# Another slot list for the first pair of a mixture-of-experts layer, with GpSimd's weight combinations moved

## The chip, the cores and the metric

The kernel runs on one core of a Trainium2 chip. A core has a matrix engine (TensorE, PE in the profile; its weight loads are PEld), a vector engine (VectorE, DVE), a scalar engine (ScalarE, ACT), GpSimd (POOL) and a sync engine (SP) that here only issues DMAs. Each engine works through its own queue in order; semaphores make one wait for another. The metric is the device time of one execution in microseconds (us), the median of several.

## The reference

All in float32. B = 8 samples, T = 512 tokens, H = 256; 64 context rows a sample; E = 3 experts with hidden width 512.

```python
nx = layer_norm(x, ln_gamma, ln_beta)
q, k, v = nx @ Wq, context @ Wk, context @ Wv
weights = softmax(q @ k.T * H ** -0.5)
evidence = weights @ v
combined = concatenate([nx, evidence, broadcast(cond)], axis=-1)
router_probs = softmax(combined @ router_W + router_b)
h = silu(einsum('btc,ecr->bter', combined, e_w1) + e_b1)
expert_out = einsum('bter,erh->bteh', h, e_w2) + e_b2
routed = sum(expert_out * router_probs[..., None], axis=-2)
g = sigmoid(silu(combined @ gate_w1 + gate_b1) @ gate_w2 + gate_b2)
return x + g * (routed @ out_w + out_b)
```

## The kernel before

The eight samples go in four pairs. For a pair, a layer's two samples and two halves of the features form a 2 by 2 block product, which is done with seven products in place of eight (Strassen's scheme with Winograd's sums). The operands of the seven are sums of activations (tile `T`) and sums of weights (`ws`, `gw2s`, `w2s`). The sums of weights are made on GpSimd by `combine` (lines 250 to 253, four operations each): `combine_weights(g)` for the first layers, `combine_gate` for the gate's second layer, `combine_second` for the experts' second layer. That second layer is multiplied beforehand by `out_w` into `w2o`: this is done once, in the first pair, by `transpose_second` (VectorE) and `second_layer` (TensorE, ScalarE), six units.

`gate_layer(j)` makes the gate's first layer of pair j up to the sums of x. Then `half_layers(j)` makes the experts' first layers (groups n = 1 to 6) and finishes the gate (n = 0). Its products are cut in two halves of 64 rows of the matrix engine, which run side by side on its upper and lower half. The order is written out by hand: a list of 57 slots, each with one product for each half, and behind the bar the steps that other engines are given at that point. The first pair has a list of its own, `SLOTS_0`, because it also holds set-up work; then `UNITS_0`, steps around the six units; then `LATE_0`, three groups of steps run in `outputs`. `HOME_0` names the bank of PSUM of each sum (eight banks). A sum that takes over a bank must wait until the earlier one has been read.

The tokens: `P1.3` is product 1 of group 3, `U`, `V`, `Y`, `Z`, `W` the parts from the evidence. `k` copies a sum (ScalarE, line 886), `a` adds one to h (VectorE, line 883), `s` is the silu (ScalarE, line 877), `w` weighs h with the router's probabilities `pb` (VectorE, line 920), `df` subtracts one weighed block from another (line 917). `lp` and `lg` are the x part of the router's logits of this pair and of the next (line 638), `rl` their evidence part (lines 751, 754), `rs` and `rx` add them up and take exponents, and `r` makes the probabilities and sends them out: `spread_probabilities` writes them to DRAM with four DMAs (`pd`, line 796) and reads them back spread over all partitions with one (`pb`, line 800), all from GpSimd's queue. `g0` to `g3` are sums for the gate's second layer (line 1229), `b2` prepares a bias (lines 564 to 569), `lx` loads the next pair's x, `st`, `dev`, `nm` are its statistics, deviation and normalization (lines 581, 585, 595), `xd` and `xg` store and reload it, `l1` and `l2` load the second weights of experts 1 and 2, `t0` to `t5` transpose them, `xb` loads x for the output. `c2` and `cg` are `combine_weights(2)` and `combine_gate`.

Each of these calls only appends instructions to its engine's queue. A GpSimd step, say, runs as soon as GpSimd's queue reaches it and its operands are there, whatever slot it is written in; the place in the list sets the order within each queue. In the setup, `end_softmax` gives GpSimd a copy of one column of the softmax's result (`wake_t`) ahead of its next work, so that this work starts after the softmax.

Of the kernel before, what the change touches and what calls it, by code (L numbers as in the profile page):

```python
# [8 lines left out]
F32 = mybir.dt.float32  # L9
# [7 lines left out]
def kernel(  # L17
# [51 lines left out]
    nc = tc.nc  # L69
    P = 128  # L70
    B, T, H = x.shape
    CT = context.shape[1]
    E, C3, RH = e_w1.shape
    KH = H // P
# [25 lines left out]
    def bank(i, name):  # L100
        ps = psum.tile([P, 512], F32, tag=f"b{i}", name=name)
        bank_of[ps.name] = i
        return ps

    def spares(*banks):
        spare[:] = banks
# [11 lines left out]
    eps_t = const.tile([P, 1], F32, tag="eps_t", name="eps_t")  # L118
    warm_t = const.tile([P, 1], F32, tag="warm_t", name="warm_t")

    wake_t = const.tile([P, 1], F32, tag="wake_t", name="wake_t")

    def load_table(func):
        nc.scalar.activation(warm_t, warm_t, func)
# [73 lines left out]
    r = 0  # L198
# [263 lines left out]

    def late_anchors():

        ps = bank(1, "ps_ar")
        for g in range(E):
            turned(ps, condT, wa[g], g * P)
        turned(ps, b2T, ow_sb, E * P)
        blocks = work.tile([P, T], F32, tag="yb", name="ar_blocks")
        n = E * P + KH * QB  # L470
        nc.vector.transpose(blocks[:, :n], ps[:, :n])
        for g in range(E):
            ar[g] = blocks[:, g * P : (g + 1) * P]
        ar["b2"] = blocks[:, E * P : n]
# [61 lines left out]

    def second_layer(u):
        e, i = u // 2, 2 * (u % 2)
        ps = bank((4, 7, 6, 5)[u % 4], f"ps_w2o_{u}")
        for d in range(2):  # L540
            for k in range(KH):
                c = k * H + d * P
                nc.tensor.matmul(  # L543
                    ps[:, d * H : (d + 1) * H], w2["T"][u % 2][:, c : c + P], ow_sb[:, k, :],
                    start=(k == 0), stop=(k == KH - 1),
                )
        c = e * RC + i
        nc.scalar.copy(w2o[:, c : c + 2, :].rearrange("p c n -> p (c n)"), ps)
        if i:
            combine_second(e)  # L550
# [371 lines left out]
    def gate_layer(j, steps):  # L922
# [96 lines left out]
    }  # L1019

    SLOTS_0 = (
        "P1.1 Z.1 |",
        "Y.1 Z.0 |",
        "P1.3 P1.1 | lp0.0 a10.0",
        "Y.0 W.0 | k00.1 lp0.1 s10.0 lp0.2",
        "P2.1 P1.3 | w11.0",
        "P4.0 P5.1 | a00.0 k00.3 s11.0 lp0.3",
        "P6.1 P2.1 | lp1.0 s00.0 lp1.1",
        "P5.1 Z.2 | a00.1",
        "U.0 P6.1 | lp1.2 k11.1 lp1.3 lx l1 l2 c2 cg s00.1",  # L1030
        "P1.2 P5.2 | rl k10.1",
        "Y.2 P4.0 | b2",
        "P5.2 P1.2 | s01.0",
        "P2.3 P3.1 | k00.2 k11.2 rs",
        "P7.1 V.1 | g0 rx",
        "P2.2 Z.3 | st0.0 st0.1",
        "P6.2 P7.1 | st0.2 st0.3",
        "Y.3 P5.3 | a11.1",
        "P3.1 P6.2 | r s11.1",
        "P6.3 V.2 | st1.0 k10.2 a10.1",  # L1040
        "P5.3 P3.2 | st1.1 s10.1",
        "U.1 P2.2 | st1.2 k11.3 st1.3",
        "P3.2 P2.3 | a00.2 dev",
        "P1.6 P6.3 | g1 a00.3",
        "P7.2 P3.3 | a10.2",
        "P4.1 P1.6 | g2",
        "P2.4 P7.2 | g3 k10.3 nm0.0 k00.6",
        "P1.5 P4.1 | nm0.1 a11.2 s00.2",
        "P1.4 V.3 | nm0.2 s01.1 nm0.3 xd0",
        "P7.3 P1.5 | nm1.0 s00.3 nm1.1 nm1.2 s10.2",  # L1050
        "P3.3 P1.4 | nm1.3 xd1 xg w00.1 k00.5",
        "P6.6 Z.6 | a10.3 k00.4",
        "P4.2 P7.3 | s11.2 w10.1 w11.1 s10.3",
        "U.2 P6.6 | a11.3",
        "P6.5 Z.4 | k10.6 w00.2 s11.3 w01.1",
        "P6.4 P4.2 | w00.3",
        "Y.4 P6.5 | s01.2 w10.2",
        "U.3 P6.4 | w11.2 k10.5 w10.3",
        "P4.3 P2.4 | k10.4 w11.3",
        "Y.6 P5.4 | a00.4 w01.2",  # L1060
        "P7.5 P4.3 | s00.4 lg0.0",
        "P5.4 P5.6 | w00.4 s01.3 lg0.1",
        "P7.4 Z.5 | k11.4 w01.3",
        "P5.6 P5.5 | lg0.2 lg0.3",
        "Y.5 P7.4 | lg1.0 k11.6 lg1.1",
        "P5.5 P7.5 | lg1.2 a11.4",
        "P2.5 P3.4 | k11.5 lg1.3 s11.4 df.1",
        "P7.6 V.6 | a11.5 t0",
        "P2.6 P3.6 | w11.4 s11.5",
        "U.4 V.5 | df.2 w11.5",  # L1070
        "P3.6 P7.6 | df.3",
        "U.5 P3.5 | a11.6 a10.6 t1",
        "P4.5 V.4 | s11.6 s10.6 w11.6",
        "P4.4 P2.5 | w10.6",
        "U.6 P4.5 | a00.5",
        "P4.6 P4.4 | s00.5 s01.5",
        "P3.4 P2.6 | w00.5 s01.4 w01.5",
        "P3.5 P4.6 | a00.6",
    )
    UNITS_0 = (  # L1080
        "a10.4 s01.6 s10.4",
        "t2 a10.5 s00.6",
        "w01.4 t3 s10.5 xb0 xb1",
        "w01.6 w00.6 t4",
        "w10.4 t5",
        "w10.5",
    )
    LATE_0 = ("", "", "df.6 df.4 df.5")
    HOME_0 = {
        "U.0": 0, "Z.0": 2, "Y.0": 3, "W.0": 1, "U.1": 4, "Z.1": 5, "Y.1": 6, "U.3": 7, "Z.2": 2,  # L1090
        "U.2": 1, "Y.2": 3, "Y.3": 6, "Z.3": 0, "U.6": 5, "Y.4": 3, "U.5": 6, "U.4": 2, "Z.6": 4,
        "Z.4": 0, "Y.6": 1, "Z.5": 3, "Y.5": 7,
    }

    def half_layers(j):
# [23 lines left out]
        def half(token, k):  # L1119
# [21 lines left out]
            "rs": lambda: router_logits(j),  # L1141
            "rx": lambda: router_exp(j),
            "b2": lambda: second_bias(),
            "c2": lambda: combine_weights(2),
            "cg": lambda: combine_gate(),
            "lx": lambda: [load_x(b) for b in (2, 3)],
            **{f"l{e}": lambda e=e: load_second(e) for e in range(1, E)},
# [60 lines left out]
                step(token)  # L1208
        if not j:
            for u, tokens in enumerate(UNITS_0):  # L1210
                second_layer(u)
                for token in tokens.split():
                    step(token)
        S["late", j] = [lambda t=tokens: [step(x) for x in t.split()] for tokens in late]

    gate_sums = {}
# [207 lines left out]
    with tc.manual_schedule(engines=None):  # L1424
# [63 lines left out]
        def end_softmax():  # L1488
            sum_weights(0)
            softmax(0)  # L1490
            nc.gpsimd.tensor_copy(wake_t, S["w", 0][:, 0, 0, 0:1])
            value_differences(0, 0)
            turn_weights(0)
            anchor_columns(E)
            combine_x(0, nc.vector, (3,))
            combine_weights(0)
            router_column()
            spread_router_bias()
            spread_router_rows(0)
            combine_weights(1)  # L1500

        def end_setup():
            value_differences(0, 1)
# [5 lines left out]
        for j in range(NP):  # L1509


            within, between = {}, {}

            def put(where, n, step, *args):
                where.setdefault(n, []).append(lambda: step(*args))

            spares(7, 5)
            if j == 0:
                spares(4, 5, 7)
                copies = []  # L1520

                def value_product(g):
                    value_weights(0, g, lambda *args: copies.append(args), False)

                def copy_values():
                    nc.scalar.copy(*copies.pop(0))

                put(within, 1, value_product, 0)
                put(within, 1, begin_softmax)
                put(within, 5, copy_values)  # L1530
                put(within, 6, load_table, AF.Silu)
                put(within, 3, value_product, 1)
                put(within, 3, copy_values)
                put(within, "sums", end_softmax)
                put(within, 7, value_product, 2)
                put(within, 7, copy_values)
                put(within, 7, end_setup)
            else:
                put(within, 3, value_weights, j, 1, nc.scalar.copy, False)
            if j + 1 < NP:  # L1540
                b0, b1 = 2 * j + 2, 2 * j + 3
                if j + 2 < NP:
                    put(between, "begin", load_x, b0 + 2)
                    put(between, "begin", load_x, b1 + 2)
                put(between, "begin", transpose_blocks, b0)
                put(between, "gate", regroup_x, b1)
                put(between, "begin", value_weights, j + 1, E)
                put(between, "begin", store_router_rows, j + 1)
                put(between, "begin", spread_router_rows, j + 1)
                put(between, "P5", transpose_blocks, b1)  # L1550
                put(between, "P6", value_weights, j + 1, 2)
                put(between, "P2", scores, j + 1)
                put(between, "P2", exponents, j + 1)
                put(between, "P2", combine_x, j + 1, nc.gpsimd)
                put(between, "P7", softmax, j + 1)
                put(between, "P7", value_weights, j + 1, 0)
                put(between, "P7", evidence_logits, j + 1)
                put(between, "P7", router_logits, j + 1)
                put(between, "P3", turn_weights, j + 1)
                put(between, "P3", router_exp, j + 1)  # L1560
            gate_layer(j, within)
            half_layers(j)
            outputs(j, between)

# [33 lines left out]
```

## Time and profile before

| what | us |
|---|---|
| median of 3 runs | 461.6 (460.97 to 461.93) |
| the profiled execution, own time | 461.67 |
| its span, first to last instruction | 459.3 |
| TensorE busy in the span | 451.5 |
| VectorE busy | 364.0 |
| ScalarE busy | 214.1 |
| GpSimd busy | 100.7 |
| first pair: first slot of its list starts | 33.99 |
| first pair: second weights' units start | 87.20 |
| first pair: the gate's second layer starts | 98.16 |

The span is what the profiler's instruction records cover; the execution's own time has in addition what lies before and after. Times in a profile row are the start from the beginning of the span and the duration. In brackets stands the idle time of the engine before the row and what ended it: `[1.05 <-DVE h L883]` is 1.05 us of idle ended by VectorE's operation of line 883 that wrote h. A row with x8 merges eight like instructions. The records of matmuls overlap by their pipeline, so a matmul of 0.59 us is followed by the next after 0.43.

### The profile page before, as it was taken

How to read it: one execution, taken by the hardware profiler on the slowest of the kernel's cores; microseconds unless marked ns; L12 is line 12 of the kernel's file. 1: busy time of each engine (PE TensorE's matmuls, PEld its weight loads, DVE VectorE, ACT ScalarE, POOL GpSimd, SP SyncE). 2: the span in 40 equal slices, each digit the busy share in tenths (PEclk: the TensorE clock that was granted, in tenths of full speed). 3: DMA queues.
4: the chain of work that ended last, by engine and by line, in shares of the span. 5: the costliest groups of instructions: out<-in, count | busy, mean ns of one | idle time of the engine just before them, and what ended most of it. 6: DMA issues, size and time to landing. Idle time of an engine off the chain costs nothing.

```text
span 459.3 us, 5502 instructions
## 1 busy us (share of the span) xinstructions
PE 451.5 (98%) x1797; PEld 216.6 (47%) x1797; DVE 364.0 (79%) x683; ACT 214.1 (47%) x373; POOL 100.7 (22%) x148
## 2 busy tenths in 40 slices
PE   8999989999999999999999999999999999999996
PEld 7544346664444444444444444444444444444445
DVE  2879989958689999479779999678869837677983
ACT  2545675556221576468220476568130456558000
POOL 5458500081062400001053300001044300000010
PEclk9999999999999999999999999999999999999999
DMA  8975572262011377403011368102011381000014
GB/s 261 385 158 125 91 230 47 47 137 46 7 23 23 48 233 124 103 0 47 7 23 23 48 204 138 28 0 46 7 23 23 48 213 17 1 0 0 1 16 76
DMA packets 119379, 35.31 MB, mean 77 GB/s; under 512 B 106012, under 2 KB 116312, under 8 KB 118840
## 3 DMA queue, kind: packets, MB, share of 16 engines
q1 hardware_dynamic: 115344, 27.02, 29.0%
q0 software_dynamic: 2080, 7.16, 4.7%
q10 hardware_dynamic: 1928, 0.80, 0.6%
q8 instruction: 14, 0.23, 0.2%
q14 instruction: 13, 0.11, 0.1%
HBM read 27.56 MB, written 7.39 MB: 76 GB/s over the span
## 4 chain that ended last, share of the span: by engine, by line
PE 90%; DMA 4%; DVE 3%; SPq 1%; issue 1%; POOL 0%; DVEq 0%; POOLq 0%
PE ps_u L841 40%; PE ps_z L841 19%; PE ps_y L841 12%; PE ps_vw L816 5%; PE ps_gu L841 3%; PE ps_w2o L543 2%; DMA pb<-pd 2%; PE ps_s L687 2%; PE ps_gz L841 1%; DMA scr_w<-in_L_xcond_Wv_dram 1%; PE ps_tokens L841 1%; PE ps_v L352 1%; PE ps_m L352 1%; PE ps_gy L841 1%; DVE junk L638 1%
## 5 line engine op out<-in xcount | busy, mean ns | idle before, releaser
L841 PE MATMUL ps_u<-nxT,w 64*128 64x512 f32 (+1 forms) x208 | 96.7, 591 | 0.0
L920 DVE TENSOR_TENSOR h<-h,pb 128x512 f32<-128x512 f32 x96 | 63.8, 696 | 18.0 <-ACT h L877 12.1
L877 ACT ACTIVATE h<-h,abias 128x512 f32<-128x512 f32 x72 | 49.5, 717 | 34.5 <-DVE h L883 34.5
L841 PE MATMUL ps_u<-h,w2o 128*128 128x512 f32 x144 | 64.2, 595 | 0.0
L841 PE MATMUL ps_z<-wT,vw 64*128 64x512 f32 x104 | 52.4, 591 | 1.3 <-DVE h L883 1.3
L841 PE MATMUL ps_z<-nxT,ws 64*128 64x512 f32 (+1 forms) x104 | 52.4, 590 | 0.0
L841 PE MATMUL ps_z<-T,ws 64*128 64x512 f32 (+1 forms) x104 | 51.6, 591 | 0.0
L841 PE MATMUL ps_y<-nxT,w 64*128 64x512 f32 (+1 forms) x104 | 51.5, 590 | 0.0
L1329 POOL TENSOR_TENSOR yb<-yb,xb 128x512 f32<-128x512 f32 x14 | 17.7, 1266 | 148.7 <-DVE yb L1328 131.6
L841 PEld LDWEIGHTS ps_u<-nxT,w 64*128 64x128 f32 (+1 forms) x208 | 37.0, 187 | 25.7 <-issue 22.6
L841 PE MATMUL ps_u<-T,ws 64*128 64x512 f32 (+1 forms) x104 | 48.7, 591 | 0.0
L841 PE MATMUL ps_u<-T,w 64*128 64x512 f32 x112 | 48.7, 589 | 0.0
L841 PE MATMUL ps_z<-h,w2s 128*128 128x512 f32 x96 | 42.5, 592 | 0.0
L841 PEld LDWEIGHTS ps_u<-h,w2o 128*128 128x128 f32 x144 | 27.0, 190 | 32.7 <-issue 30.9
L886 ACT COPY h<-ps_u 128x512 f32<-128x512 f32 x48 | 27.6, 579 | 22.6 <-PE ps_u L841 22.6
L1296 DVE TENSOR_TENSOR h<-h,h 128x1024 f32<-128x1024 f32 x24 | 34.3, 1485 | 0.0
L429 POOL DMA_DIRECT2D vrd<-vw x8 | 5.0, 627 | 114.2 <-ACT vw L823 111.6
L841 PE MATMUL ps_u<-wT,vw 64*128 64x512 f32 x56 | 28.3, 594 | 1.1 <-DVE h L883 1.1
L841 PEld LDWEIGHTS ps_z<-h,w2s 128*128 128x128 f32 x96 | 18.2, 190 | 23.0 <-issue 22.3
L841 PE MATMUL ps_y<-wT,vw 64*128 64x512 f32 x56 | 28.3, 595 | 0.0
L816 PE MATMUL ps_vw<-w,vT 128*128 128x512 f32 (+1 forms) x64 | 26.7, 539 | 0.0
L841 PEld LDWEIGHTS ps_y<-nxT,w 64*128 64x128 f32 (+1 forms) x104 | 19.4, 187 | 13.6 <-issue 13.4
(230 smaller groups left out, 822.6 us busy)
## 6 DMA issues: line engine op xcount, KB each, us to landing
pb<-pd POOLq DMA_DIRECT2D x4, 1536.0 KB, 7.4
xb<-in_x_dram SPq DMA_DIRECT2D x64, 64.0 KB, 2.4
out_dram<-yb SPq DMA_DIRECT2D x56, 64.0 KB, 1.9
x<-in_x_dram SPq DMA_DIRECT2D x24, 128.0 KB, 2.9
xd<-x SPq DMA_DIRECT2D x24, 128.0 KB, 2.2
xg<-xd SPq DMA_DIRECT2D x48, 64.0 KB, 2.3
w<-in_L_xcond_e_w_dram SPq DMA_DIRECT2D x4, 512.0 KB, 6.8
scr_wa<-in_L_xcond_e_w_dram SPq DMA_DIRECT2D x3, 512.0 KB, 9.1
```

The lines of the kernel that those rows point to most:

```text
L352: nc.tensor.matmul(ps, w_sb[:, k, m * P : (m + 1) * P], src[:, k, :], start=(k == 0), stop=(k == KH - 1))
L429: nc.gpsimd.dma_start(S["vrd", j][i].rearrange("e c -> c e"), S["vw", j][row_half(i), R0:])
L543: nc.tensor.matmul(ps[:, d * H : (d + 1) * H], w2["T"][u % 2][:, c : c + P], ow_sb[:, k, :], start=(k == 0), stop=(k == KH - 1),)
L638: nc.vector.scalar_tensor_tensor(junk, S["xn", b][:, t, :], 1.0, gg, ALU.mult, ALU.mult, accum_out=sums[:, t : t + 1])
L687: nc.tensor.matmul(ps[side(i, h), g * NH : (g + 1) * NH], mr[:, k, 2 * j + i, g * TB : (g + 1) * TB], S["nxT", 2 * j + i][:, k, h * NH : ( ...
L816: nc.tensor.matmul(ps, vT[:, k, j * 2 * CT : (j + 1) * 2 * CT], w1[:, KH + k, n0:n1], start=(k == 0), stop=(k == KH - 1),)
L841: return nc.tensor.matmul(ps, lhsT, rhs, start=start, stop=True, skip_group_check=not start)
L877: nc.scalar.activation(h, h if src is None else src, AF.Silu, bias=abias[:, c, 2 * j + i : 2 * j + i + 1])
L886: nc.scalar.copy(chunk(n, i, d), part)
L920: nc.vector.tensor_tensor(h, h, S["pb", j][:, i, :, 2 * q // RC, :], ALU.mult)
L1296: nc.vector.tensor_tensor(d, p, m, ALU.subtract)
L1329: nc.gpsimd.tensor_tensor(yb, yb, S["xb", 2 * j + row][:, i, :], ALU.add)
```

## The change

1. `SLOTS_0`, `UNITS_0`, `LATE_0` and `HOME_0` are replaced. The new list has 57 slots with the same products and the same kinds of steps in another order. The first weighing (`w00.2`) stands in slot 33; before it was `w00.1`, in slot 29; `b2` stands in slot 24 instead of 10, `r` in slot 18 instead of 17, three router parts of the next pair (`lg0.0` to `lg0.2`) ahead of the first weighing. All six `df` stand in the last group of `LATE_0` instead of three.
2. `c2` and `cg` stand in slot 16 instead of 8. Ahead of `c2` GpSimd gets a copy of one column of the next pair's statistics (`gpsimd_behind`), which those statistics have to be made for. `wake_t` is renamed `behind_t` and goes through the same function.
3. In `end_softmax`, `combine_weights(1)` stands ahead of `spread_router_bias` and `spread_router_rows` instead of behind.
4. `l1` and `l2` stand in slot 28 instead of 8.
5. In `UNITS_0` the steps of a unit stand ahead of its matmuls instead of behind, and the banks of the units, of `late_anchors` and of the spare sums are others; the blocks of `late_anchors` lie in tile `xg` instead of `yb`.

```diff
+    def gpsimd_behind(column):
+
+        nc.gpsimd.tensor_copy(behind_t, column)
...
     def late_anchors():
 
-        ps = bank(1, "ps_ar")
+        ps = bank(7, "ps_ar")
...
-        blocks = work.tile([P, T], F32, tag="yb", name="ar_blocks")
+        blocks = work.tile([P, KH, T], F32, tag="xg", name="ar_blocks", bufs=1)[:, 0, :]
...
-        ps = bank((4, 7, 6, 5)[u % 4], f"ps_w2o_{u}")
+        ps = bank((4, 6, 7, 3)[u % 4], f"ps_w2o_{u}")
...
-        "U.0 P6.1 | lp1.2 k11.1 lp1.3 lx l1 l2 c2 cg s00.1",
-        "P1.2 P5.2 | rl k10.1",
-        "Y.2 P4.0 | b2",
...
-        "P3.1 P6.2 | r s11.1",
-        "P6.3 V.2 | st1.0 k10.2 a10.1",
-        "P5.3 P3.2 | st1.1 s10.1",
-        "U.1 P2.2 | st1.2 k11.3 st1.3",
...
-        "P3.3 P1.4 | nm1.3 xd1 xg w00.1 k00.5",
-        "P6.6 Z.6 | a10.3 k00.4",
-        "P4.2 P7.3 | s11.2 w10.1 w11.1 s10.3",
-        "U.2 P6.6 | a11.3",
-        "P6.5 Z.4 | k10.6 w00.2 s11.3 w01.1",
...
+        "P5.2 V.1 | lp1.3 lx s01.0 rl",
...
+        "P6.2 P1.3 | a10.1",
+        "P2.3 V.2 | st0.0 c2 cg st0.1",
+        "P7.1 P6.2 | st0.2",
+        "P1.5 Z.3 | st0.3 k00.3 r k10.2",
+        "P3.2 P7.1 | s00.2 st1.0",
+        "Y.3 P1.5 | a10.2 s10.1",
+        "P6.3 P1.6 | a11.1 s10.2 st1.1 k00.5",
+        "P7.2 P2.3 | st1.2 k00.6 st1.3",
+        "P1.4 P6.3 | s11.1 a00.3",
+        "P4.1 P7.2 | dev b2",
...
+        "U.2 P4.1 | nm0.0 k10.5 nm0.1 l1 l2",
...
+        "P5.4 P6.6 | s11.2 lg0.0 lg0.1 s01.2",
+        "P2.4 V.3 | lg0.2 k10.6 w00.2",
+        "P6.4 P3.3 | k11.4 w00.1",
+        "Y.4 P7.3 | w01.1 w10.1",
+        "P3.3 P6.4 | a11.3",
+        "Y.6 V.4 | k10.4 a10.3 s11.3 w11.1",
+        "P2.6 P3.4 | w00.3 s10.3",
+        "U.3 P2.4 | w10.2",
+        "P3.4 P5.6 | w11.2 a00.4",
+        "P7.6 Z.6 | a10.4 s00.4",
+        "P7.4 P2.6 | w01.2 s10.4 w11.3",
+        "P7.5 P7.6 | a00.6",
+        "P2.5 P7.4 | w10.3 t0 s00.6",
+        "Y.5 Z.5 | w00.4 a11.4",
+        "P5.6 P5.5 | w10.4 s11.4",
+        "P4.3 P7.5 | w00.6 k11.6 w11.4",
+        "P5.5 P2.5 | a11.6 t1",
+        "U.4 P4.3 | k11.5 a00.5 s11.6",
+        "P4.4 P3.6 | a11.5 s01.3 w11.6",
+        "U.6 V.6 | s00.5 w01.3",
...
-    LATE_0 = ("", "", "df.6 df.4 df.5")
+    LATE_0 = ("", "", "df.1 df.2 df.3 df.4 df.5 df.6")
...
-            "c2": lambda: combine_weights(2),
+            "c2": lambda: (gpsimd_behind(S["mv", 1][:, 0, 0, 0:1]), combine_weights(2)),
...
             for u, tokens in enumerate(UNITS_0):
-                second_layer(u)
                 for token in tokens.split():
                     step(token)
+                second_layer(u)
...
             combine_weights(0)
             router_column()
+            combine_weights(1)
             spread_router_bias()
             spread_router_rows(0)
-            combine_weights(1)
...
-                spares(4, 5, 7)
+                spares(4, 5, 1)
```

## The prediction

> **What bounds the kernel now.** I read the shares of busy time, then the busy time by stages, then the first pair's matmuls, then what VectorE does just before their gaps, then GpSimd's row.
>
> ```profile
> PE 451.5 (98%) x1797; PEld 216.6 (47%) x1797; DVE 364.0 (79%) x683; ACT 214.1 (47%) x373; POOL 100.7 (22%) x148
> ...
> 34.00:51.50 17.50, 17.43 (x86) 7.65 (x80) 16.68 (x46) 9.35 (x14) 14.34 (x31) 1.00 0.62 122
> 51.50:66.40 14.90, 12.57 (x56) 5.81 (x56) 12.58 (x35) 10.75 (x19) 2.70 (x6) 1.00 0.59 163
> 66.40:87.20 20.80, 20.80 (x95) 11.80 (x95) 19.95 (x46) 9.89 (x17) 0.00 (x0) 1.00 0.32 62
> 87.20:98.20 11.00, 10.92 (x50) 9.09 (x50) 9.83 (x18) 6.51 (x12) 6.42 (x7) 1.00 0.55 93
> 153.70:202.80 49.10, 49.10 (x230) 21.97 (x229) 41.23 (x95) 30.41 (x48) 3.61 (x7) 1.00 0.50 113
> ```
>
> Columns after the stretch: its length, then busy TensorE, weight loads, VectorE, ScalarE, GpSimd. TensorE is the bound of the kernel at full clock (1.00); only where it waits is there time to win. The last row is the second pair's list of 57 slots: 49.1 us, TensorE never idle. The first pair's list, also 57 slots, fills the first three rows: 53.2 us, with VectorE almost as full as TensorE.
>
> ```profile
> 33.99 0.69 PE L841 MATMUL ps_u<-nxT,w 64*128 64x512 f32 x1
> ...
> 34.53 0.59 PE L841 MATMUL ps_u<-nxT,w 64*128 64x512 f32 x1
> ...
> 34.96 0.59 PE L841 MATMUL ps_y<-wT,vw 64*128 64x512 f32 x1
> ...
> 52.49 0.69 PE L841 MATMUL ps_u<-wT,vw 64*128 64x512 f32 x1 [1.05 <-DVE h L883]
> ...
> 66.36 0.69 PE L841 MATMUL ps_z<-wT,vw 64*128 64x512 f32 x1 [1.34 <-DVE h L883]
> ...
> 87.20 11.13 PE L543 MATMUL ps_w2o<-ow_sb,w2T 128*128 128x256 f32 x48
> 98.16 1.02 PE L841 MATMUL ps_gu<-hg,gw_sb 128*128 128x512 f32 x2
> ```
>
> A half product is two passes, and passes follow each other at 0.4285 us (34.53, 34.96), so a slot is 0.857 us. Floor of the stretch: 57 x 0.857 = 48.87, and the second weights' 48 passes of 256 columns at half of 0.4285 = 10.29; together 59.16. Measured from 33.99 to 98.16: 64.17. So 5.01 us are lost here, and that is all this change can win. Subtracting slot number x 0.857 from the start of each slot shows where: 0.11 at the start, 1.23 at slot 20 (52.49), 0.38 in slots 21 to 24, 2.05 at slot 33 (66.36), 0.40 at slot 53, 0.17 into the second weights, 0.67 within them.
>
> ```profile
> 45.39 0.38 DVE L564 COPY b2o<-ar_blocks 128x6 f32<-128x6 f32 x1
> 45.81 1.44 DVE L566 TENSOR_SCALAR b2o<-b2o 128x2 f32<-128x2 f32 x2
> 47.28 0.55 DVE L569 TENSOR_TENSOR b2o<-b2o,cols 128x2 f32<-128x2 f32 x1
> ...
> 51.74 0.69 DVE L883 TENSOR_TENSOR h<-h,ps_u 128x512 f32<-128x512 f32 x1 [0.19 <-issue]
> ...
> 65.02 0.69 DVE L920 TENSOR_TENSOR h<-h,pb 128x512 f32<-128x512 f32 x1 [1.82 <-DMA pb<-pd]
> 65.63 0.68 DVE L883 TENSOR_TENSOR h<-h,ps_z 128x512 f32<-128x512 f32 x1
> ...
> 53.52 2.02 POOL L796 DMA_DIRECT2D pd<-prT  x4 [3.38 <-DVE prT L793]
> 57.27 0.56 POOL L800 DMA_DIRECT2D pb<-pd  x1 [1.73 <-DMA pd<-prT]
> ```
>
> The slot-20 gap ends with the add of 51.74 (a11.1): VectorE had worked from 34.13 without a real gap and was late. The slot-33 gap ends with the add of 65.63 (a10.3), queued behind a weighing that waited 1.82 us for the spread probabilities pb. The four b2 operations work on two to six columns and took 2.37 us because GpSimd's combinations (45.11 to 50.14) ran beside them.
>
> **The change, part by part.** *New list.* No product, add or weighing is added or dropped; the floor stays 59.16. I add up VectorE's queue in the new order, from the same start 34.13. Prices per row: an add or weighing 0.60 (distance of neighbouring rows), a router part 0.46, one statistics step 0.54 (four from 49.34 to 51.5), `rl` 2.77 (42.62 to 45.39), `rs` 0.97, `r` 0.84, `t` 0.69, the set-up before the first add 2.0.
>
> First gate: slot 23 opens a bank that add a10.2 must have read. Before it stand set-up 2.0, seven adds 4.2, eight router parts 3.7, `rl` 2.8, `rs` 1.0, five statistics 2.7, `r` 0.8: 17.2, so 51.35, and some 0.7 of idle for sums TensorE has not yet made: 52.1. TensorE comes at 34.1 + 23 x 0.857 = 53.8. In the old list b2 and g0 stood before a11.1, needed at 51.2; now both stand behind. The gaps of slots 20 to 24 go: 1.6 us.
>
> Second gate: the weighings. The probabilities go through GpSimd's queue: pd, then pb. The new list puts the eight combinations (`c2 cg`) ahead of pd and holds them with a one-column copy until the first statistics are there: 13.7 of the same prices, so 48.5. Copy 0.2 to 0.44 (the same copy took 0.44 at 26.91), combinations 45.11 to 50.14 less 0.59 for one that met a VectorE operation (1.00 against 0.45 beside it): 4.4. pd starts at 53.1 to 53.4; before, 53.52. pb is thus no earlier than 0.1 to 0.4 us, and the first weighing starts at 64.8 instead of 65.02, VectorE arriving about 63.5 and idle again. What changes is what waits behind it. Old: a10.3, needed at slot 33. New: four weighings, then a11.3, done at 64.8 + 4 x 0.60 + 0.68 = 67.9; slot 39 wants it at 67.5. The tightest is a11.6 for slot 51: 15 weighings, six adds, one `t`, itself: 21 x 0.602 + 0.69 + 0.68 = 14.0, so 78.8 against 34.1 + 51 x 0.857 = 77.8. I take 1.05 us lost, the 0.4 within it. From there VectorE has ten adds and weighings, four router parts and `t1` up to `t2`, 8.6 us, against TensorE's six slots and two units, 8.6: another 0 to 0.5; I take 0.3. With 0.11 at the start and 0.15 into the second weights: 1.6 left of 5.0.
>
> *GpSimd beside other work.* b2 falls from 2.37 to four times 0.15 (the neighbouring 128x32 rows: 0.44 for three). Moving `combine_weights(1)` ahead of four DMAs frees two router parts (0.84 and 0.74 against 0.41) and puts its four operations beside `abias` and `vw`: minus 0.8, plus up to 0.8; I take 0. Behind it wait the `rbias` and `vr` DMAs: 2.9 us later (35.14 to 38.35, less the overlap), landing near 41 (2.9 from issue by the median row), needed by `rl` at 42.9 by the sum. Without that cover `rl` would lose what it is late.
>
> *DMAs.* SP's order is unchanged (x, then both second weights, then xd): the tokens `l1 l2` stand later in the list, but nothing that SP waits for lies between, so sixteen issues leave as before. Nothing.
>
> *Three more subtractions (`df`) behind the second weights:* 3 x 0.60 = 1.8 at about 105, where VectorE was idle 0.78 and then ran ahead of experts starting at 110.44. It ends 1.4 before them. Nothing, or 0.4 if the transposes slip. Other banks and tiles: no added instruction, nothing.
>
> The row against a rule: pd's four issues cost 0.505 each and pb 0.56 with statistics and adds beside them. The Trainium skill (SBUF — State Buffer, "SBUF: two separate sides") says that a VectorE copy or scalar operation in its two-port mode locks GpSimd out of writing the descriptors of its own DMAs, with 620 ns becoming 3100 ns in its measurement. That speaks against this change, since b2 now stands near 55 (52.1 plus two adds and three statistics), between pd and pb. By the page, an estimate of 2.5 us on pb, and a result near 460.7; no row here shows it.
>
> **Sum.** 459.3 - (5.0 - 1.6) = 455.9 span. The profiled execution took 461.67, 2.4 more than its span; the median is 461.6. Forecast: 461.6 - 3.4 = 458.2 us.
>
> **Rivals.** *Nearly the floor* (14%): pb lands 1 us sooner (7.73 us here from issue, 7.4 the median row; pd released sooner), slot 51 waits for nothing, 0.4 lost: 457.0. For: the later pairs reach it. Against: pd's place behind the combinations.
> *Given back on GpSimd, slower* (9%): the eight combinations and the copy stand ahead of pd; if each meets a two-input VectorE operation as the 1.00 us one did (+0.55 each: 4.4) and the first statistics come 0.7 late, pb is 5 us later, slot 51 starts 6.1 late and all is lost: 1.1 slower, 462.7. It decides from 3.4 us of delay on. For: GpSimd was slowed in 35.88 to 38.35 too. Against: the statistics rows at 49.34 to 50.9 ran at full speed beside it.
> *Traded evenly* (9%): delay of 3 to 4 us, by that or the page's rule: 461.3.
>
> **How the numbers follow.** Forecast 68% (457.4 to 459.5). From no change this kernel's measurement tells about 0.2%, 0.9 us. Faster: 68 + 14 and a little of the even case, 83%; same 8%; slower 9%. Range 456.8 to 460.7: the floor case at the low end, half the gain lost to pb or a late gate at the high end.
>
> **What would show it.** First product of the second weights at 84 (87.20 before); no gap before slot 50; pd at 53.2; a gap of about 1 us ended by an h add near 78; b2 below 1 us. Wrong if pd starts after 55, or if a gap stands in slots 5 to 25: then the sum of VectorE's queue is short.

## The result, and the profile after

| what | before | after |
|---|---|---|
| median of 5 runs, us | 461.34 (460.97 to 461.93) | 456.93 (456.88 to 457.35) |
| profiled execution, own time / span | 461.67 / 459.3 | 456.89 / 455.0 |
| first slot starts | 33.99 | 33.23 |
| gate's second layer starts | 98.16 | 93.83 |
| stretch between the two | 64.17 | 60.60 |
| span behind it | 361.14 | 361.17 |

The ratio is 0.9905, 95% interval 0.9891 to 0.9920: 4.4 us faster, where 3.4 were forecast. The stretch of the first pair gives 3.57 of it. First the busy times and the chain of waits on the page of the changed kernel, then its first pair by stages (length, then busy TensorE, weight loads, VectorE, ScalarE, GpSimd):

```profile
PE 450.1 (99%) x1797; PEld 214.5 (47%) x1797; DVE 360.2 (79%) x683; ACT 214.0 (47%) x373; POOL 99.1 (22%) x149
...
PE 98%; DMA 1%; ACT 0%; DVE 0%; ACTq 0%; issue 0%
```

```profile
34.00:51.50 17.50, 17.50 (x84) 7.89 (x82) 15.30 (x50) 10.52 (x16) 10.98 (x28) 1.00 0.61 123
51.50:66.40 14.90, 14.90 (x74) 6.64 (x70) 13.57 (x39) 12.06 (x21) 3.75 (x9) 1.00 0.65 198
66.40:84.00 17.60, 17.60 (x80) 9.19 (x77) 17.50 (x39) 9.04 (x14) 0.00 (x0) 1.00 0.38 61
84.00:94.50 10.50, 10.50 (x48) 8.74 (x47) 6.98 (x15) 5.14 (x9) 6.22 (x8) 1.00 0.39 74
```

TensorE is busy through the second row, where it had been idle 2.33 us (12.57 of 14.90). VectorE's wait for pb and the longest gap left to TensorE in the list stand here:

```profile
63.64 2.50 DVE L924 TENSOR_TENSOR h<-h,pb 128x512 f32<-128x512 f32 x4 [0.95 <-DMA pb<-pd]
66.06 0.68 DVE L887 TENSOR_TENSOR h<-h,ps_u 128x512 f32<-128x512 f32 x1
...
76.92 0.68 DVE L887 TENSOR_TENSOR h<-h,ps_u 128x512 f32<-128x512 f32 x1
```

```profile
76.57 0.66 PE L845 MATMUL ps_z<-nxT,ws 64*128 64x512 f32 x1
76.77 0.59 PE L845 MATMUL ps_u<-T,w 64*128 64x512 f32 x1
77.07 0.59 PE L845 MATMUL ps_z<-nxT,ws 64*128 64x512 f32 x1
77.65 0.69 PE L845 MATMUL ps_u<-wT,vw 64*128 64x512 f32 x1
...
93.83 1.02 PE L845 MATMUL ps_gu<-hg,gw_sb 128*128 128x512 f32 x2
```

The first weighing still waits for pb, 0.95 us. From 40.5 to the second weights this is the only idle time of VectorE that the view shows. Counted against 0.857 us a slot, TensorE loses 0.11 at the start, 0.14 at slot 39 (the add of 66.06), 0.47 at slots 50 and 51 (a11.6, the add of 76.92, lets the matmul of 77.65 start), 0.13 at slot 53 and 0.59 into and within the second weights: 1.44 in place of 5.01.

GpSimd's queue and the four b2 operations:

```profile
47.95 0.19 POOL L125 COPY behind_t<-mv 128x1 f32<-128x1 f32 x1 [3.05 <-DVE mv L586]
48.10 0.64 POOL L254 TENSOR_TENSOR ws<-w 128x256 f32<-128x256 f32 x1
...
52.15 0.46 POOL L257 TENSOR_TENSOR gw2s<-gw_sb,gw2s 128x128 f32<-128x128 f32 x1
52.54 2.03 POOL L800 DMA_DIRECT2D pd<-prT  x4
56.30 0.56 POOL L804 DMA_DIRECT2D pb<-pd  x1 [1.73 <-DMA pd<-prT]
```

```profile
54.40 0.17 DVE L568 COPY b2o<-ar_blocks 128x6 f32<-128x6 f32 x1
54.60 0.36 DVE L570 TENSOR_SCALAR b2o<-b2o 128x2 f32<-128x2 f32 x2
54.99 0.16 DVE L573 TENSOR_TENSOR b2o<-b2o,cols 128x2 f32<-128x2 f32 x1
```

The copy held the combinations until the first statistics were done (47.82); pd follows the eighth with no idle time. b2 runs after them and takes 0.69 us (0.17, 0.36, 0.16), where it took 2.37.

### The profile page after: what moved, and what is told of

It reads as the page before. It is cut to its first block, busy times and chain, and to the rows that moved or that the text cites. A ratio compares the mean times of both kernels' runs of the same rounds, so it can differ in the third digit from the quotient of the medians.

```text
span 455.0 us, 5502 instructions
## 1 busy us (share of the span) xinstructions
PE 450.1 (99%) x1797; PEld 214.5 (47%) x1797; DVE 360.2 (79%) x683; ACT 214.0 (47%) x373; POOL 99.1 (22%) x149
## 4 chain that ended last, share of the span: by engine, by line
PE 98%; DMA 1%; ACT 0%; DVE 0%; ACTq 0%; issue 0%
PE ps_u L845 45%; PE ps_z L845 20%; PE ps_y L845 14%; PE ps_vw L820 5%; PE ps_gu L845 3%; PE ps_w2o L547 2%; PE ps_s L691 2%; PE ps_gz L845 2%; PE ps_tokens L845 1%; PE ps_v L356 1%; DMA scr_w<-in_L_xcond_Wk_dram 1%; PE ps_m L356 1%; PE ps_gy L845 1%; PE pt_x L619 0%; PE ps_kq L369 0%; PE ps_ar L456 0%
## 5 line engine op out<-in xcount | busy, mean ns | idle before, releaser
L924 DVE TENSOR_TENSOR h<-h,pb 128x512 f32<-128x512 f32 x96 | 62.6, 684 | 16.3 <-ACT h L881 11.1
```

Source lines behind the costliest of these rows:

```text
L924: nc.vector.tensor_tensor(h, h, S["pb", j][:, i, :, 2 * q // RC, :], ALU.mult)
```

## The experiments

All runs are read with one sum. From the gate's second layer to the end of the span every kernel here takes 361.13 to 361.22 us. What comes before is the start of the list, the time from there to the first weighing, and from the first weighing to the gate ("tail"):

| kernel | median us | ratio to before, 95% | start | to first weighing | tail | stretch |
|---|---|---|---|---|---|---|
| before | 461.34 | | 33.99 | 31.03 | 33.14 | 64.17 |
| before_gpsimd | 459.01 | 0.9948 (0.9936 to 0.9961) | 33.48 | 28.50 | 33.14 | 61.64 |
| before_swap | 460.87 | 0.9990 (0.9981 to 0.9999) | 33.26 | 31.33 | 32.53 | 63.86 |
| before_gpsimd_swap | 458.19 | 0.9933 (0.9918 to 0.9948) | 33.78 | 28.87 | 32.54 | 61.41 |
| before_df | 460.80 | 0.9988 (0.9979 to 0.9996) | 33.31 | 31.08 | 32.61 | 63.69 |
| before_gpsimd_swap_df | 457.34 | 0.9911 (0.9898 to 0.9925) | 33.78 | 28.44 | 31.75 | 60.19 |
| after | 456.93 | 0.9905 (0.9891 to 0.9920) | 33.23 | 30.41 | 30.19 | 60.60 |
| after_old_gpsimd | 456.62 | 0.9896 (0.9881 to 0.9911) | 33.67 | 30.14 | 30.19 | 60.33 |
| after_old_b2_early | 457.97 | 0.9928 (0.9913 to 0.9943) | 33.34 | 31.56 | 30.19 | 61.75 |
| after_pd_late | 458.79 | 0.9950 (0.9937 to 0.9962) | 33.37 | 32.02 | 30.19 | 62.21 |
| after_cg_behind | 457.08 | 0.9914 (0.9899 to 0.9928) | 33.60 | 29.85 | 30.19 | 60.04 |
| after_df | 459.28 | 0.9954 (0.9937 to 0.9971) | 34.67 | 30.84 | 32.00 | 62.84 |
| after_lg8 | 457.28 | 0.9908 (0.9895 to 0.9922) | 33.35 | 29.80 | 29.96 | 59.76 |
| after_cg_lg8 | 456.70 | 0.9897 (0.9882 to 0.9913) | 33.45 | 30.15 | 29.96 | 60.11 |

Each ratio is against executions of the old kernel in the same round; their median was 461.20 to 461.34. The start moves from run to run whatever the list (33.23 to 34.67), so parts of the lists are compared by the stretch. The tail comes out equal to 0.01 us wherever the order behind the first weighing is the same. The other two columns come from one profiled execution of each kernel, and the executions of one kernel have spans that differ (455.0 to 455.5 for the changed kernel, 454.6 to 456.8 for after_cg_behind): a difference of a few tenths in them, with no difference of the tail, is not shown by these profiles.

**before_gpsimd**: the old list, GpSimd's part of the change alone.

```diff
-        "U.0 P6.1 | lp1.2 k11.1 lp1.3 lx l1 l2 c2 cg s00.1",
+        "U.0 P6.1 | lp1.2 k11.1 lp1.3 lx l1 l2 s00.1",
...
-        "P2.2 Z.3 | st0.0 st0.1",
+        "P2.2 Z.3 | st0.0 c2 cg st0.1",
...
-            "c2": lambda: combine_weights(2),
+            "c2": lambda: (nc.gpsimd.tensor_copy(wake_t, S["mv", 1][:, 0, 0, 0:1]), combine_weights(2)),
...
+            combine_weights(1)
             spread_router_bias()
             spread_router_rows(0)
-            combine_weights(1)
```

> The kernel before with its own list of slots; only GpSimd's part of the change is made: the gate's and second weights' combinations go behind the first statistics (slot 14), with the one-column copy that holds them, and combine_weights(1) ahead of the spreading DMAs. Theory (the new list brings most of the 4.4 us, by what stands ahead of and behind each waiting VectorE operation): the four b2 operations fall from 2.37 to below 1 us, so the gap of slots 20 to 24 shrinks, but the second weighing-bound gap near slot 33 stays at 1.5 to 2 us: about 1.3 us faster than before, 460.0 us. Rival (the gain is that GpSimd and VectorE no longer meet): most of the gain shows here too, 457.5 us, and the gap at slot 33 is below 0.5 us.

Half of the gain shows, more than the theory's 1.3 us and less than the rival's. Its VectorE and GpSimd rows:

```profile
44.20 0.16 DVE L564 COPY b2o<-ar_blocks 128x6 f32<-128x6 f32 x1
44.39 0.36 DVE L566 TENSOR_SCALAR b2o<-b2o 128x2 f32<-128x2 f32 x2
44.79 0.16 DVE L569 TENSOR_TENSOR b2o<-b2o,cols 128x2 f32<-128x2 f32 x1
...
51.58 2.02 POOL L796 DMA_DIRECT2D pd<-prT  x4
55.34 0.56 POOL L800 DMA_DIRECT2D pb<-pd  x1 [1.74 <-DMA pd<-prT]
...
61.98 0.69 DVE L920 TENSOR_TENSOR h<-h,pb 128x512 f32<-128x512 f32 x1 [1.86 <-DMA pb<-pd]
```

VectorE reaches b2 10.72 us after the start instead of 11.40 and does it in 0.68 us instead of 2.37; the gap of slot 20 is gone. pb is issued 21.86 us after the start instead of 23.28 and used after 28.50 instead of 31.03. The tail is the old 33.14: the whole gain of 2.53 us is the earlier weighing, 1.42 of it by the earlier issue and 1.11 by a shorter transfer (6.64 us from issue to use instead of 7.75), whose reason is open. By this sum the gap at slot 20 was worth nothing by itself: had pb not come earlier, the list would have ended as late as before. The product that waits at slot 33 starts 29.84 us after the list (63.32) where it had started after 32.37; its gap is about 1.1 us, neither theory's figure.

**after_old_gpsimd**: the new list, GpSimd's part put back.

```diff
-        "P5.2 V.1 | lp1.3 lx s01.0 rl",
+        "P5.2 V.1 | lp1.3 lx c2 cg s01.0 rl",
...
-        "P2.3 V.2 | st0.0 c2 cg st0.1",
+        "P2.3 V.2 | st0.0 st0.1",
...
-            "c2": lambda: (gpsimd_behind(S["mv", 1][:, 0, 0, 0:1]), combine_weights(2)),
+            "c2": lambda: combine_weights(2),
...
-            combine_weights(1)
             spread_router_bias()
             spread_router_rows(0)
+            combine_weights(1)
```

> The changed kernel with its new list; only GpSimd's part is put back: the combinations stand at slot 10 with no copy to hold them, and combine_weights(1) behind the spreading DMAs. Theory (the list brings most): about 1.0 us slower than the changed kernel, 457.9 us, lost in several small gaps of 0.2 to 0.5 us, the first already before slot 25 because rl, rs or statistics meet the combinations. Rival (no more meeting is what counts): 460 us or more, that is at least 3 us of the 4.4 are gone.

Neither holds: nothing is lost. In its profile the stretch is even 0.27 us shorter: pb is issued 0.90 us earlier after the start, as the combinations no longer hold pd up, and its transfer takes 0.63 longer. So the list alone brings the whole gain, and GpSimd's part alone half of it: they do not add up.

**after_old_b2_early**: that kernel with b2 put ahead of `rs`, beside the combinations (`dev b2` becomes `dev`, `rs` becomes `b2 rs`).

> The changed kernel's list with GpSimd's part put back (456.6 us when run) and b2 moved back early, to slot 13, ahead of rs: the four b2 operations then stand beside GpSimd's combinations again, as they did before. Theory (the new list and GpSimd's part each remove the same meeting; in the new list it is gone because b2 stands behind the combinations): b2 takes above 2 us again instead of 0.67, prT and so pd and pb come 1.2 to 2 us later, and the first weighing with them: 458.0 to 458.6 us. Rival (the meeting costs nothing that TensorE waits for): 456.6 us, within 0.4.

```profile
45.39 0.38 DVE L568 COPY b2o<-ar_blocks 128x6 f32<-128x6 f32 x1
45.80 1.45 DVE L570 TENSOR_SCALAR b2o<-b2o 128x2 f32<-128x2 f32 x2
47.29 0.56 DVE L573 TENSOR_TENSOR b2o<-b2o,cols 128x2 f32<-128x2 f32 x1
```

b2 takes 2.39 us again, the weighing comes 1.42 later (31.56 against 30.14) and the stretch is 1.42 longer. So each of the two parts removes the same meeting: the one moves the combinations, the other b2.

**after_pd_late**: the hold is on the fourth statistics column (`mv[:, 0, 3]`) instead of the first, `c2 cg` stand directly ahead of `r`.

> The changed kernel with GpSimd's eight combinations held behind the last of the first four statistics instead of the first, so that pd starts about 1.7 us later and nothing else is moved. Theory (pb sets slot 51): the first weighing starts about 1.7 us later (65.3), slot 51's lag grows from 0.72 to about 2.3 us, 458.4 us. Rival (pb is not on the path that sets the end): at most 0.3 us, 457.2 us, with the lag at slot 51 as before.

```profile
65.39 2.50 DVE L924 TENSOR_TENSOR h<-h,pb 128x512 f32<-128x512 f32 x4 [2.36 <-DMA pb<-pd]
67.80 0.68 DVE L887 TENSOR_TENSOR h<-h,ps_u 128x512 f32<-128x512 f32 x1
...
68.54 0.69 PE L845 MATMUL ps_u<-wT,vw 64*128 64x512 f32 x1 [1.42 <-DVE h L887]
```

As the theory had it, the weighing comes 1.61 later from the start and the stretch is 1.61 longer. It shows already at slot 39, whose add (67.80) stands behind four weighings. In the new list pb's delay is paid one for one.

**after_cg_behind**: `cg` moved from behind `c2` to behind `r`, so behind pd and pb on GpSimd's queue.

> The changed kernel with the four combinations of the gate (cg) behind the router's spreading DMAs pd and pb on GpSimd's queue instead of ahead of them; the second weights' four (c2) stay ahead. Theory (pb is what the last gap, 0.47 us at slot 50, waits for): pd starts 1.6 to 2.0 us earlier than 52.54, the first weighing about 62.3 instead of 63.64, the lag of slot 51 falls from 0.72 to 0.3 us or less: 456.3 us. Rival (the gap at slot 50 is VectorE's own sum of work, pb only ends an idle time in it): no change, 456.9 us, or 0.3 us slower because cg now meets the two-input adds and g0 to g2 of VectorE.

```profile
51.17 2.02 POOL L800 DMA_DIRECT2D pd<-prT  x4
55.65 0.56 POOL L804 DMA_DIRECT2D pb<-pd  x1 [2.46 <-DMA pd<-prT]
56.23 0.82 POOL L254 TENSOR_TENSOR gw2s<-gw_sb 128x128 f32<-128x128 f32 x1
```

```profile
56.78 0.83 DVE L1233 TENSOR_TENSOR g_t<-hg,hg 128x512 f32<-128x512 f32 x1
57.64 0.83 DVE L1233 TENSOR_TENSOR g_t<-g_t,hg 128x512 f32<-128x512 f32 x1
...
63.45 2.49 DVE L924 TENSOR_TENSOR h<-h,pb 128x512 f32<-128x512 f32 x4
```

```profile
DMA to landing us min/median/max: 6.6/6.6/6.6
```

pd goes 1.74 us earlier from the start, pb 1.02, as pd took longer to land (2.46 of waiting, not 1.73). The last row is the landing of pb: issued at 55.65, it was there at 62.2, about where the theory had the weighing. But the weighing's row has no bracket: VectorE itself arrives 1.25 us after pb, at 63.45, partly because two of the gate's sums take 0.83 us each beside `cg` instead of 0.69. So the weighing comes only 0.56 earlier from the start, and here VectorE's work ahead of it, not pb, sets it. The gap at slot 51 is gone and the stretch is 0.56 shorter, as the lag theory asked; the rival's meeting of `cg` with the gate's sums shows too. The median does not tell this kernel from the changed one.

**before_swap** and **before_gpsimd_swap**: the old list with the first weighing behind the add that slot 33 waits for, with GpSimd's part of old and of new.

```diff
-        "P3.3 P1.4 | nm1.3 xd1 xg w00.1 k00.5",
+        "P3.3 P1.4 | nm1.3 xd1 xg k00.5",
-        "P6.6 Z.6 | a10.3 k00.4",
+        "P6.6 Z.6 | a10.3 w00.1 k00.4",
```

> The kernel before with one token moved: the first weighing (w00.1), which waits for pb, stands behind the add a10.3 instead of ahead of it (slots 29 and 30 of the old list). GpSimd's part stays as before. Theory (the gap at slot 33 is there because the add that slot needs is queued behind a weighing that waits for pb): the gap of 2.05 us near slot 33 falls below 0.5 us. Not all of it is kept, since pb comes no earlier and the adds behind the next weighings then decide slots 39 to 53: 0.6 to 1.2 us faster than before, 460.3 us. Rival (pb itself is too late for TensorE, whatever stands behind the weighing): the gap stays at 1.5 us or more, 461.2 us.

> The run with GpSimd's part alone (old list, 459.0 us) with the same one token moved as well: a10.3 ahead of the first weighing. Theory: the gap of 1.1 us that was left near slot 33 falls below 0.3 us; 0.5 to 1.0 us faster than 459.0, so 458.3 us, and what is then left against the new list (456.9) is VectorE's later order. Rival (with GpSimd's part made, the order around the weighing no longer counts): 459.0 us, with the gap as it was.

```profile
62.70 0.68 DVE L883 TENSOR_TENSOR h<-h,ps_z 128x512 f32<-128x512 f32 x1
64.59 1.90 DVE L920 TENSOR_TENSOR h<-h,pb 128x512 f32<-128x512 f32 x3 [1.21 <-DMA pb<-pd]
66.40 0.68 DVE L883 TENSOR_TENSOR h<-h,ps_u 128x512 f32<-128x512 f32 x1
...
67.14 0.69 PE L841 MATMUL ps_u<-wT,vw 64*128 64x512 f32 x1 [0.38 <-DVE h L883]
```

In before_swap (shown) the add runs ahead of the wait and slot 33's product starts 30.77 us after the list (64.03), not 32.37: 1.6 us won. But the next add (66.40) stands behind three weighings and TensorE waits for it at 67.14; of the 1.6 us 0.30 are left when the second weights start, and 0.31 at the gate. In both lists the tail falls by 0.6, no more. In before_gpsimd_swap the gap before slot 33 is gone and the median is the theory's, but of the stretch only 0.23 us are won against before_gpsimd: the transfer of pb took 7.00 us there, not 6.64, and a gap of 0.4 us stands at slot 36. One add put ahead of the wait moves the gap, it does not remove it.

**before_df** and **before_gpsimd_swap_df**: `df.1` to `df.3` leave the old list for the last group of `LATE_0`. **after_df**: they go back into the new one (shown; the last group of `LATE_0` then keeps the other three).

```diff
-        "Y.5 Z.5 | w00.4 a11.4",
+        "Y.5 Z.5 | w00.4 df.1 a11.4",
...
-        "P5.5 P2.5 | a11.6 t1",
+        "P5.5 P2.5 | df.2 a11.6 t1",
-        "U.4 P4.3 | k11.5 a00.5 s11.6",
+        "U.4 P4.3 | k11.5 a00.5 s11.6 df.3",
```

> The kernel before with one thing changed: the subtractions df.1 to df.3 are taken out of its list (slots 45, 48 and 49) and put behind the second weights, where the change puts them. Theory (VectorE's work after the first weighing, not the one add behind it, sets the end of the stretch; 3 x 0.60 = 1.8 us of it go): what is lost after the gap at slot 33, 1.24 us before, falls to 0.3 or less; the gaps at slots 20 and 33 stay: 0.7 to 1.0 us faster than before, 460.4 us. Rival (as the forecast had it, the move of df is worth nothing): 461.3 us, within 0.2.

> The old list with three small edits and nothing else of the new list: GpSimd's part, a10.3 ahead of the first weighing, df.1 to df.3 behind the second weights. Theory (these three are what the new list brings, and they add up since each acts on another stage): the stretch from the first slot to the gate layer, 61.41 us without the df move, falls by 0.7 to 1.2 us to 60.2 to 60.7, as in the changed kernel (60.60): 457.2 us, the same as the changed kernel within 0.4. Rival (the rest of the new order matters by itself): 458.2 us, as without the df move.

> The changed kernel with the three subtractions df.1 to df.3 put back into the list (slots 45, 48 and 49, as far along as they stood before) instead of behind the second weights. Theory (from the first weighing on VectorE has no slack up to slot 51 and little after, so every VectorE operation ahead of a11.6 and of the last units costs its length): the lag at slot 51 grows from 0.72 us to 1.8 or more, and the whole is 1.5 to 1.8 us slower, 458.5 us. Rival (VectorE has slack there and their place is worth nothing, as the forecast had it): 456.9 us, within 0.4.

```profile
76.39 0.68 DVE L921 TENSOR_TENSOR h<-h,h 128x512 f32<-128x512 f32 x1
...
79.39 0.68 DVE L921 TENSOR_TENSOR h<-h,h 128x512 f32<-128x512 f32 x1
80.00 0.68 DVE L887 TENSOR_TENSOR h<-h,ps_u 128x512 f32<-128x512 f32 x1
...
80.73 0.69 PE L845 MATMUL ps_u<-wT,vw 64*128 64x512 f32 x1 [0.59 <-DVE h L887]
```

In after_df two subtractions stand ahead of a11.6 (80.00), which TensorE waits for; the tail grows from 30.19 to 32.00, 1.81 us for three operations of 0.60: their full length. In the old list alone they are worth 0.5 (less than the theory's 0.7 to 1.0), all of it in the second weights; with the other two edits the tail falls by 0.79 (32.54 to 31.75), and the other 0.43 of that stretch's 1.22 is the transfer of pb (6.59 us instead of 7.00). The old list with these three edits has a stretch of 60.19 us, and its median lies 0.41 us from the changed kernel's, about as expected there: the three bring 4.0 of the 4.4 us. But they get there by another way. The weighing comes 1.97 us earlier after the start than in the changed kernel, 0.75 of it by the shorter transfer, and the tail is 1.56 longer. What else of the new order shortens the tail is not shown.

**after_lg8** and **after_cg_lg8**: the eight router reductions of the next pair move from the list to the first group of `LATE_0`, where VectorE had been idle 5.08 us.

> The changed kernel with only the eight reductions lg0.0 to lg1.3 moved behind the second weights; GpSimd's queue is not touched. Theory (here pb, not VectorE's sum, decides slot 51, and the reductions stand in VectorE's idle time ahead of pb or behind slot 51): the first weighing stays at 63.6 with a longer wait ahead of it (2 us or more), the lag at slot 51 stays, and only 0.1 to 0.4 us are won in the second weights: 456.6 us. Rival (VectorE's whole work up to the last second weight is the limit, wherever it stands): 1 us or more faster than the changed kernel, 455.8 us.

> The changed kernel with two edits: the gate's combinations (cg) behind pd and pb on GpSimd's queue, and the eight reductions lg0.0 to lg1.3, which only the second pair's router reads, taken out of the list and put behind the second weights, where VectorE was idle for 5.08 us. Theory (with pb 1.4 us earlier VectorE's own sum of work limits slot 51 and the second weights; eight reductions of 0.46 us leave it): first weighing at 62.8 or before, no lag above 0.3 us up to slot 51, stretch 59.4 to 59.7 us against 60.04 for the cg edit alone and 60.60 for the changed kernel: 455.9 us. Rival (TensorE is already the bound of what is left): 60.04 as with the cg edit alone, 456.7 us.

The tail falls by 0.23 in both. The rest is pb: in after_cg_lg8 it was used 8.10 us after its issue, so the early issue (55.50) brought nothing and this theory failed; the median is the rival's, but with pb this late its reason is not tried; in after_lg8 the same transfer took 6.73, 0.61 less than in the changed kernel, and accounts for the rest of the 0.84. The other three executions of after_lg8 had spans 0.8 to 1.1 us longer than the profiled one, and its median is no better than the changed kernel's. No run was faster than the changed kernel by more than the intervals.

## Why the prediction was right

- *First gate*: the gaps of slots 20 to 24 are gone, and slot 39 is the first to lose anything, as worked out. But its 1.6 us is not a term of its own: before_gpsimd shows that it counts only as far as the weighing comes earlier too. The sum held because the second gate was counted from TensorE's new, earlier arrival.
- *Second gate*: on the forecast's clock (the list started 0.76 us later) pd is at 53.30 (forecast 53.1 to 53.4) and the first weighing at 64.40 (64.8). The difference is that pb was used 7.34 us after its issue, not 7.75. So slots 39 to 51 lose 0.61, not 1.05. The place was right, the size half an us too large; the second weights lose 0.72 against 0.45 forecast.
- *What waits behind the weighing*: true, but too narrow. before_swap shows that the one add is not enough. What counts is how many VectorE operations stand between pb and the next adds that TensorE needs. The new list lets TensorE run to slot 39 before it needs one, and has six operations fewer between the first weighing and the last second weight: three df, which after_df prices at 1.81 us, and three lg. For the lg it is not shown: taking the five away that the new list has there cut the tail by 0.23 us (after_lg8).
- *GpSimd beside other work*: b2 at 0.69 us against 0.6; none of the eight combinations was slowed; `combine_weights(1)` cost nothing in the list, and the two DMAs behind it left 1.98 us later on the forecast's clock, not 2.9, since GpSimd had stood idle for 1.26 us ahead of them before. What was not foreseen: in the new list the whole part is worth nothing (after_old_gpsimd), since b2 was already out of the way.
- *DMAs*: the x and second-weight issues of SP start at 39.61, 44.30 and 48.50, against 40.30, 44.42 and 48.62; nothing, as said.
- *df*: "nothing, or 0.4" was the wrong price. The prediction looked at where they went and not where they left: the sum of VectorE's queue had their absence in it, unnamed, and after_df prices it at 1.81 us.
- *The rule on two-port operations* (the Trainium skill, SBUF — State Buffer, "SBUF: two separate sides"): with b2 between pd and pb, pd's four issues took 2.03 us and pb's 0.56, as before (2.02, 0.56). This does not test the rule: b2 ran from 54.40 to 55.15, beside the end of the fourth issue alone (to 54.57) and then in GpSimd's wait for pd. The estimate of 2.5 us did not come.
- *Rivals*: the floor case asked for 0.4 us lost; the measured 1.44 lies close to the likeliest case's 1.6. Neither of the delays on GpSimd came; after_pd_late shows what one would have cost, 1 us for 1 us. By that the slower rival's own sum is short: a delay of 5 us, less the 3.4 of the forecast, is 1.6 us slower, not 1.1.
- *The rest of the 4.4*: 3.57 is the stretch (forecast 3.4). In the profiled executions 0.76 lies ahead of the first slot, where the first product waited 0.78 us for the load of Wv before and for nothing after. The variants' starts overlap (old list 33.26 to 33.99, new list 33.23 to 34.67; in after_df the same wait is 1.62), so this is no shown effect of the change. What lies outside the span was 1.85 to 1.93 us in five runs after and 1.95 to 2.46 before, at the median some 0.4 less; that goes with the kernel, and why is open. So the number is in part luck: the median lies below the likeliest case's own band (457.4 to 459.5) and on the floor rival's 457.0, while the stretch went as the likeliest case had it.

## What to carry to other kernels

Where one late transfer splits an engine's queue, price the order in two numbers: when the first operation that needs the transfer starts, and how much work of that engine stands between it and each sum that the bound engine needs; gaps of the bound engine ahead of it are no terms of their own. Take work off that second part, or give the bound engine sums that need none of it, before tuning the transfer. Two edits that remove the same meeting are worth one of them: try each alone before adding their prices, and price a moved operation at the place that it leaves as well.

## What the runs showed of the hardware

- Operations of two to six columns in SBUF lost much beside GpSimd's two-input operations: b2 took 2.37 and 2.39 us there, 0.69 and 0.68 in two kernels away from them, while a statistics row ran at 0.39 to 0.40 beside the same combinations. The router reductions, moved beside GpSimd's work in after_lg8, took 0.82 to 0.95 in place of 0.42 (two rows below). The Trainium skill (SBUF — State Buffer, "Who interferes with whom") has the rule: VectorE operations with two inputs from SBUF, and copies and scalar operations in two-port mode, share a port pair with GpSimd. The rows with two inputs agree, and so do the statistics, which have one; whether b2's copy and scalar operations ran in that mode no row shows.

```profile
91.55 0.79 POOL L255 TENSOR_TENSOR w2s<-w2s,w2o 128x256 f32<-128x256 f32 x1
91.79 0.82 DVE L642 SCALAR_TENSOR_TENSOR junk<-x,gg 128x256 f32<-128x256 f32 x1
```

- The same 1.5 MB transfer of pb was used between 6.59 and 8.10 us after its issue wherever VectorE waited for it, without a simple relation to when it was issued: issued at 55.3 to 55.7 it took 6.59 to 7.00 in three kernels with the old list, issued at 55.84 and 55.50 it took 7.97 and 8.10 in two with the new, and issued at 55.65 it landed after 6.6 in a third with the new (after_cg_behind). What it meets on the way was not tried. The difference is as large as what the kernels with the new order have left to win over the floor of 59.16 (0.6 to 1.4 us).
